# A transformer block on one core: first loads, tables, shared buffers and engine order laid out anew

## The chip, the cores and the metric

The kernel runs on one core of a Trainium2 chip. The core has engines that work side by side and wait for each other through semaphores: TensorE (PE in the profile, with its weight loads as PEld), VectorE (DVE), ScalarE (ACT), GpSimd (POOL) and SyncE (SP, which issues transfers). Transfers run on 16 DMA engines. The metric is device time in microseconds, and lower is better.

## The reference

The input x has the shape (16, 128, 96, 96) in f32: 16 images of 128 channels and 96 x 96 pixels. It passes one block of channel attention and one feed-forward part with a depthwise convolution:

```
xn1 = layernorm over channels(x)
q, k, v = xn1 @ wq.T, xn1 @ wk.T, xn1 @ wv.T         # 8 heads of 16 channels
q, k = l2norm over the pixels(q), l2norm(k)
attn = softmax(q k^T * 16^-0.5)                      # 16 x 16 for each head
x = x + (attn v) @ wp.T
xn2 = layernorm over channels(x)
h1 = w_in xn2                                        # 128 -> 512 channels
h2 = depthwise 3x3 convolution(h1, w_dw)             # padding 1
h3 = gelu(h2)
x = x + w_out h3                                     # 512 -> 128 channels
```

All of it is in f32.

## The kernel before

The channels lie on the 128 partitions, the pixels along the free axis. An image is cut into 8 bands of 12 rows (BR), a band into 3 units of 4 rows (UPB units of UR rows). The 512 hidden channels are 4 chunks of 128.

For each image there is a first pass (names with `_a`): a band of x is loaded (`load`, SP), turned to pixels x channels by PE transposes (`forth`), DVE takes the statistics (`stats`), POOL turns the variance into the factor of the layer norm (`variance`, `power`), the pixels are scaled (`scaled`, by POOL, or for the first image by DVE straight from PSUM, `direct`), PE sums the Gram matrix (`gram`), and the scaled pixels are turned back into the ring buffer xn (`back` on PE, `place` on ACT). `attention` makes from the Gram matrix one 128 x 128 matrix mwT for the image in a chain of short steps over PE, ACT, DVE and POOL. The second pass (`_b`) multiplies xn by mwT (`mix`), adds x, takes the layer norm again and writes xn.

`conv_job` is one chunk of one band: PE makes the hidden rows (`hidden`), ACT copies them to SBUF (`kept`), ACT multiplies the rows by some taps into pr buffers (`products`), POOL adds one of these to the shifted rows in the tile merged (`merge`), DVE runs the other taps into the accumulator acc and at last into an h3 buffer (`tap`), two DMAs that accumulate, issued by POOL, add the remaining products (`add_products`, `add_h3`), and ACT takes the gelu in place. In some bands the fourth chunk runs on PE instead (`by_tiles`, 32 x 32 blocks with the diagonal matrices diag). `ffn_out` multiplies the four h3 tiles of a band by woutT (in the tiled bands by woutR, which is woutT's last chunk with its quarters turned by the unit) and adds the result to x, which SP stores.

The buffers that rotate are h3 (8), pr (8), x1 (2), xb (5), zT (4) and the four PSUM banks h. Before the first images' work, `weights` loads the weights into two h3 buffers, transposes them on PE and makes the tables on DVE: wqkT, wqk2c, winT, woutT, woutR, ratio, eye, diag, ksum, turned.

The order on each engine is written out by the program before anything is issued. Every operation is put on record with `op(engine, ns, place, work, reads, writes, ...)`; `Plan.order` runs them through a model with the durations ns and the places (the constants AT and RANK), which gives a list for each engine and each kind of buffer that several engines take; the table MOVES then shifts single entries of these lists by some positions, and `in_turn` merges the lists into one sequence. On the chip each engine takes its instructions in that sequence and waits where it must. At the start before, the order on SP's queue is: band 0 of x (L1632), wq and wk (L1486, L1487), wp (L1488), w_in, w_out (L1489, L1490), bands 1 to 5, the depthwise weights (L1586), band 6; on ACT's queue stand the four columns w1, b1, w2, b2 (L1324) and wv (L1331).

Of the kernel before, what the change touches and what calls it, by code (L numbers as in the profile page):

```python
# [36 lines left out]
FOURTH_TAP = 6  # L37
LAST_TAP, TOP_LAST, END_LAST = 8, 6, 2
# [11 lines left out]
H3_BUFS = 8  # L50
# [7 lines left out]
    load_w=-10068.713, weights=-247.64243, zeros=-5822.3994, load_a=-41.673394, forth_a=-1466.3766,  # L58
# [2184 lines left out]
```

## Time and profile before

| | |
|---|---|
| median of 3 runs | 3874.92 us (3870.5 to 3881.82) |
| the profiled execution, time | 3873.51 us |
| its span, first to last instruction | 3871.5 us |
| mean granted TensorE clock | 0.991 |
| busy, PE / DVE / ACT / POOL | 3701.4 / 3707.3 / 3570.9 / 3291.6 us |
| DMA, packets' time as a share of 16 engines | 81.2% (issued by POOL), 11.1% (issued by SP) |
| median time to land of an accumulating DMA | 7.4 us (into pr), 7.7 us (into h3) |

How to read the rows: `0.80 0.38 SPq L1632 DMA_DIRECT2D x<-in_x_dram x1` is an instruction at 0.80 us that took 0.38 us, on SP's queue, from line 1632, which writes x from the input; in square brackets stands how long its engine had been idle before it, and what ended that. A row of waits gives the total in us, how many there were, and the longest. A row of groups gives the count, then the busy time in us with the mean of one in ns, then the idle time before them. A row of a stretch gives its two ends and its length, the busy us of PE, PEld, DVE, ACT and POOL with the number of instructions, the granted clock, the busy share of the DMA engines and their GB/s. "issue" is time in which nothing that the profile shows was waited for.

### The profile page before, as it was taken

Reading aid. Unit: us, or ns where it says so; the run is one execution under the profiler, and the core shown is the slowest. Engines: PE = TensorE matmul, PEld = TensorE weight load, DVE = VectorE, ACT = ScalarE, POOL = GpSimd, SP = SyncE. Lnnn points to the kernel's source line nnn. Section 1 sums busy time; section 2 is a strip of 40 time slices with the busy share of each in tenths; the row PEclk is TensorE's granted clock in tenths of the full one; section 3 lists DMA queues with packets and bytes.
Section 4 is the critical chain, followed back from the end, with each engine's and each line's share of the span. In section 5 each row is a group of like instructions: output and inputs, shape, how many; then the busy total and the mean of one; then the engine's idle time right before and its main releaser. Section 6 shows DMA issues by size and latency. Waiting matters only on the chain. (4 is left out here: it accounts for less than half of the span.)

```text
span 3871.5 us, 73795 instructions
## 1 busy us (share of the span) xinstructions
PE 3701.4 (96%) x28244; PEld 2380.4 (61%) x28244; DVE 3707.3 (96%) x4242; ACT 3570.9 (92%) x5444; POOL 3291.6 (85%) x3053
## 2 busy tenths in 40 slices
PE   8999999999999999999999999999999999999987
PEld 6566666666666656656666666666666566665554
DVE  6999999999999999999999999999999999999997
ACT  2999999999999999999999999999999999999995
POOL 5888889898898888889888898898989888887674
PEclk9999999999999999999999999999999999999998
DMA  2799999999999989999999999999999999988996
GB/s 95 166 200 210 188 207 216 197 205 204 206 203 206 195 185 223 192 195 200 197 215 198 196 208 196 200 204 205 203 190 207 196 210 201 204 186 182 198 195 145
DMA packets 186593, 757.62 MB, mean 196 GB/s; under 512 B 21632, under 2 KB 23040, under 8 KB 186240
## 3 DMA queue, kind: packets, MB, share of 16 engines
q0 software_dynamic: 146736, 601.10, 81.2%
q1 hardware_dynamic: 38784, 151.75, 11.1%
q8 instruction: 221, 3.62, 0.4%
q14 instruction: 132, 1.08, 0.1%
q10 hardware_dynamic: 720, 0.07, 0.0%
HBM read 148.85 MB, written 75.50 MB: 58 GB/s over the span
## 5 line engine op out<-in xcount | busy, mean ns | idle before, releaser
L2015 ACT ACTIVATE pr<-h,ratio 128x1152 f32<-128x1152 f32 x1440 | 1785.8, 1280 | 12.8 <-POOL merged L2018 3.5
L2031 DVE SCALAR_TENSOR_TENSOR acc<-h,ratio,acc 128x1152 f32<-128x1152 f32 (+1 forms) x1248 | 1731.9, 1388 | 15.3
L2018 POOL TENSOR_TENSOR merged<-pr,h 128x1152 f32<-128x1152 f32 x448 | 1158.1, 2585 | 137.2 <-ACT pr L2015 85.3
L1999 PE MATMUL h<-xn,winT 128*128 128x384 f32 (+2 forms) x3072 | 1191.6, 495 | 38.5 <-ACT h L2004 14.1
L2151 PE MATMUL h<-h,woutT 128*128 128x384 f32 x2688 | 993.0, 489 | 11.7 <-ACT h L2048 8.1
L2004 ACT COPY h<-h 128x384 f32<-128x384 f32 (+2 forms) x1536 | 717.5, 498 | 77.0 <-PE h L1999 70.7
L1999 PEld LDWEIGHTS h<-xn,winT 128*128 128x128 f32 x3072 | 534.8, 190 | 393.0 <-ACT h L2004 44.8
L2151 PEld LDWEIGHTS h<-h,woutT 128*128 128x128 f32 x2688 | 492.9, 190 | 336.1 <-issue 27.3
L2027 DVE SCALAR_TENSOR_TENSOR acc<-h,ratio,merged 128x1152 f32<-128x1152 f32 x448 | 664.6, 1483 | 25.2 <-POOL merged L2021 10.8
L2027 DVE SCALAR_TENSOR_TENSOR h<-h,ratio,acc 128x1152 f32<-128x1152 f32 x448 | 630.5, 1407 | 12.1 <-PE h L2151 3.1
L2048 ACT ACTIVATE h<-h,ksum 128x1152 f32<-128x1152 f32 (+2 forms) x560 | 588.1, 1080 | 48.7 <-DMA h<-pr 48.4
L2043 POOL DMA_DIRECT2D h<-pr x448 | 466.6, 1044 | 168.1 <-DVE h L2027 36.8
L2040 POOL DMA_DIRECT2D pr<-pr x448 | 469.4, 1066 | 75.2 <-ACT pr L2015 53.0
L2115 PE MATMUL h<-h,diag 32*32 32x384 f32 x13824 | 479.4, 489 | 20.2 <-issue 14.5
L2115 PEld LDWEIGHTS h<-h,diag 32*32 32x32 f32 x13824 | 278.9, 103 | 175.4 <-issue 76.0
L1722 POOL TENSOR_TENSOR ve_a<-ve_a,mhalf 128x4 f32<-128x4 f32 x288 | 359.9, 1253 | 9.4
L1746 POOL TENSOR_TENSOR zT<-zT,ve_a 128x512 f32<-128x512 f32 x270 | 357.4, 1337 | 4.2
L1705 PE MATMUL h<-ident,x 128*128 128x128 f32 x2244 | 330.7, 275 | 29.5 <-DMA x<-in_x_dram 15.7
L1722 POOL TENSOR_TENSOR ve_b<-ve_b,mhalf 128x4 f32<-128x4 f32 x288 | 351.4, 1238 | 6.7
L1705 PEld LDWEIGHTS h<-ident,x 128*128 128x128 f32 x2244 | 266.3, 141 | 147.1 <-issue 55.1
L1655 PE MATMUL h<-xn,mwT 128*128 128x384 f32 x768 | 296.8, 498 | 7.1 <-ACT h L2004 3.4
L1753 PEld LDWEIGHTS g<-zT 128*128 128x128 f32 x2160 | 273.2, 191 | 47.0 <-POOL zT L1746 8.0
(185 smaller groups left out, 4109.9 us busy)
## 6 DMA issues: line engine op xcount, KB each, us to landing
pr<-pr POOLq DMA_DIRECT2D x448, 576.0 KB, 7.4
h<-pr POOLq DMA_DIRECT2D x448, 576.0 KB, 7.7
x<-in_x_dram SPq DMA_DIRECT2D x128, 576.0 KB, 6.5
out_dram<-x SPq DMA_DIRECT2D x127, 576.0 KB, 4.4
x<-in_x_dram POOLq DMA_DIRECT2D x123, 576.0 KB, 6.6
out_dram<-x SPq DMA_DIRECT2D x3, 192.0 KB, 3.0
h<-in_L_conv_w_in_dram SPq DMA_DIRECT2D x1, 256.0 KB, 3.5
h<-in_L_conv_w_out_dram SPq DMA_DIRECT2D x1, 256.0 KB, 3.6
```

Source lines behind the costliest of these rows:

```text
L1705: nc.tensor.transpose(d["pT", q][:, k, :], xt[:, j * P : (j + 1) * P], ident)
L1722: nc.gpsimd.tensor_tensor(rstd, rstd, mhalf, ALU.pow)
L1999: nc.tensor.matmul(rows(ph), lhsT=winT[:, n, :], rhs=window(xn, r0 + r, e - r, 1), start=True, stop=True)
L2004: nc.scalar.copy(window(h1_, r, e - r, 1), rows(d.pop(("ph", r))))
L2015: nc.scalar.activation(to, shifted(t), AF.Copy, scale=ratio[:, n, t : t + 1])
L2018: nc.gpsimd.tensor_tensor(merged, d["pr", dma_taps[0]], shifted(UNIT), ALU.add)
L2027: nc.vector.scalar_tensor_tensor(to, shifted(t), ratio[:, n, t : t + 1], also, ALU.mult, ALU.add)
L2031: nc.vector.scalar_tensor_tensor(to, shifted(t)[:, lo:hi, cut], ratio[:, n, t : t + 1], to, ALU.mult, ALU.add)
L2040: nc.gpsimd.dma_start(out=d["pr", dma_taps[1]], in_=d["pr", t], accum_op=ALU.add)
L2048: nc.scalar.activation(h3, h3, AF.Gelu, bias=ksum[:, z, n : n + 1])
L2115: nc.tensor.matmul(d[s][quads[to], lo:hi, cut], lhsT=diag[quads[of], t, :], rhs=window(h1_, s * UR + dy + lo, hi - lo, dx)[quads[of], :, : ...
L2151: nc.tensor.matmul(rows(d["po"]), lhsT=woutR[:, s, :] if n == PE_CHUNK and by_pe(g) else woutT[:, n, :], rhs=h3s[g, n][:, s * UR : (s + 1) ...
```

## The change

- First loads. The four columns and wv go from ACT's queue to SP's. The weights' loads are split in two operations: `loads_qkp` (wq, wk, wp, wv, w1, b1; one h3 buffer) and `loads` (w2, b2, w_in, w_out; the other), with a place of its own for the second (`load_f`). Bands 5 to 7 of the first image are loaded into pr buffers and no longer into the two x1 buffers. The planner's extra time for the very first load (T_START) goes.
- Tables. eye, diag, turned, woutT and woutR are made by ACT and no longer by DVE, in operations of their own (`diagonals`, `turn_bias`, and `keep_out` as an ACT operation). woutR has two units and no longer three: the first one is woutT itself. ncq is gone: the operation that added it works it out.
- Shared buffers. centre lies in the free part of an h3 buffer; merged becomes a pool `mg` with one buffer.
- h3 has nine buffers and no longer eight.
- A tap on POOL is written (`pool_tap`), with POOL_TAPS empty.
- MOVES is new for every engine and for the lists h and h3, and the lists pr and x1 come in, since more than one engine now takes pr buffers.

```diff
+POOL_TAPS = ()
+MG_BUFS = 1
-H3_BUFS = 8
+H3_BUFS = 9
 AT = dict(
+    load_f=-385.2,
...
 MOVES = dict(
...
-    SP={2: -2, 6: -2, 8: -1, 36: -1, 40: -1, 52: -1, 56: -1, 60: -1, 99: -1, 104: -1, 106: -1, 120: -1, 133: -1,
...
+    SP={0: 2, 4: -1, 6: 6, 9: -1, 10: -3, 12: -3, 37: -1, 43: -1, 53: -1, 57: -1, 61: -1, 69: -1, 73: -1, 91: -1,
...
+    x1={1: -1},
+    xb={3: -1},
+    pr={0: 2, 10: -1, 13: -2, 14: -1, 17: 0, 19: -3, 20: 0, 21: -2, 22: 2, 28: 2, 34: -1, 37: -1, 40: -1, 41: 3,
...
-    xb={1: -1},
-    h3={3: -2, 7: -3, 8: -2, 9: -1},
+    h3={0: 6, 1: 4, 5: -2, 6: 2, 7: -5, 9: -8, 10: -3, 18: -1, 42: -1, 50: -1, 58: -1, 105: -1, 114: -1, 154: -1,
...
-T_START = 2300
+T_POOL_TAP = 2600
...
-    centre = const.tile([P, P], F32, name="centre")
-    nc.vector.tensor_scalar(centre, ident, -1.0 / C, None, ALU.add)
...
-        nc.scalar.dma_start(out=t, in_=v.rearrange("(c o) -> c o", o=1))
+    def column(t, v):
+        nc.sync.dma_start(out=t, in_=v.rearrange("(c o) -> c o", o=1))
...
-    nc.scalar.dma_start(out=wv_sb, in_=wv)
-    ncq = const.tile([1, P], F32, name="ncq")
-    woutR = const.tile([P, UPB, P], F32, name="woutR")
+    woutR = const.tile([P, UPB - 1, P], F32, name="woutR")
-    merged = h1p.tile([P, BR, W], F32, name="merged")
+    mg_bufs = [h1p.tile([P, BR, W], F32, name=f"mg_{k}") for k in range(MG_BUFS)]
...
         def loads():
+            column(w2, ln2_w)
+            column(b2, ln2_b)
+            nc.sync.dma_start(out=v["win"], in_=w_in.rearrange("(n p) c kh kw -> p n (c kh kw)", p=P))
+            nc.sync.dma_start(out=v["wout"], in_=w_out.rearrange("c j kh kw -> c (j kh kw)"))
+        def loads_qkp():
...
+            v["centre"] = b[:, 8 * P : 9 * P]
             nc.sync.dma_start(out=v["wqk"][:, :P], in_=wq)
             nc.sync.dma_start(out=v["wqk"][:, P:], in_=wk)
             nc.sync.dma_start(out=v["wp"], in_=wp)
+            nc.sync.dma_start(out=wv_sb, in_=wv)
+            column(w1, ln1_w)
+            column(b1, ln1_b)
...
+        def diagonals():
             for q in quads:
-                nc.vector.tensor_copy(eye[q, :], ident[q, q])
+                nc.scalar.copy(eye[q, :], ident[q, q])
             for t in range(9):
-                nc.vector.tensor_scalar(diag[:, t, :], eye, ratio[:, PE_CHUNK, t : t + 1], None, ALU.mult)
+                nc.scalar.activation(diag[:, t, :], eye, AF.Copy, scale=ratio[:, PE_CHUNK, t : t + 1])
...
+        def turn_bias():
             for s in range(UPB):
                 for to, of in zip(quads, turn(s)):
-                    nc.vector.tensor_copy(turned[to, s, :], ksum[of, :, PE_CHUNK])
+                    nc.scalar.copy(turned[to, s, :], ksum[of, :, PE_CHUNK])
 
         def keep_out(pt):
-            nc.vector.tensor_copy(woutT.rearrange("p n c -> p (n c)"), pt)
-            for s in range(UPB):
+            nc.scalar.copy(woutT.rearrange("p n c -> p (n c)"), pt)
+            for s in range(1, UPB):
                 for to, of in zip(quads, turn(s)):
-                    nc.vector.tensor_copy(woutR[to, s, :], pt[of, PE_CHUNK * P : (PE_CHUNK + 1) * P])
+                    nc.scalar.copy(woutR[to, s - 1, :], pt[of, PE_CHUNK * P : (PE_CHUNK + 1) * P])
...
-        op("SP", 1700, at("load_w", p), loads, [], mine, 2500, dma=2 * T_MOVE)
+        op("SP", 2700, at("load_w", p), loads_qkp, [], mine[1:], 2500, dma=T_MOVE)
...
+        op("SP", 1800, at("load_f", p), loads, [], mine[:1], 2500, dma=2 * T_MOVE)
+        act(2900, at("late", p), diagonals, [("w", "unit")], [("w", "diag")])
+        act(2400, at("late", p), turn_bias, [("w", "sum")], [("w", "diag")])
...
-        return "xb" if second or i == 0 and b < XB_BUFS else "x1"
+        return "xb" if second or i == 0 and b < XB_BUFS else "x1" if i else "pr"
...
-            nc.vector.tensor_add(v["sqn"], v["ps_r"][:, :P], ncq)
+            nc.vector.scalar_tensor_tensor(v["sqn"], cqk[:, :P], float(NTOK), v["ps_r"][:, :P], ALU.mult, ALU.add)
...
-                rows(d["po"]), lhsT=woutR[:, s, :] if n == PE_CHUNK and by_pe(g) else woutT[:, n, :],
+                rows(d["po"]), lhsT=woutR[:, s - 1, :] if s and n == PE_CHUNK and by_pe(g) else woutT[:, n, :],
```

More of the change, by code (lines that the diff above doesn't have):

```diff
@@ L57 @@
 AT = dict(
-    load_w=-10068.713, weights=-247.64243, zeros=-5822.3994, load_a=-41.673394, forth_a=-1466.3766,
+    load_f=-385.2, load_w=-10068.713, weights=-247.64243, zeros=-5822.3994, load_a=-41.673394, forth_a=-1466.3766,
     stats_a=14511.788, variance_a=8052.0351, power_a=-10117.23, pool_product=152.05, merge=-2414.1489,
@@ L1320, in tile_restormer_block @@
     nc.gpsimd.memset(mhalf, -0.5)
-    def column(v, name):
-        t = const.tile([P, 1], F32, name=name)
-        nc.scalar.dma_start(out=t, in_=v.rearrange("(c o) -> c o", o=1))
-        return t
-    w1, b1 = column(ln1_w, "w1"), column(ln1_b, "b1")
-    w2, b2 = column(ln2_w, "w2"), column(ln2_b, "b2")
+    w1, b1, w2, b2 = (const.tile([P, 1], F32, name=name) for name in ("w1", "b1", "w2", "b2"))
+    def column(t, v):
+        nc.sync.dma_start(out=t, in_=v.rearrange("(c o) -> c o", o=1))
     wv_sb = const.tile([P, P], F32, name="wv_sb")
-    nc.scalar.dma_start(out=wv_sb, in_=wv)
     dw = const.tile([P, NCH, 9], F32, name="dw")
@@ L1413, in tile_restormer_block @@
     plan = Plan(
-        tr=TR_BANKS, bk=BK_BANKS, h=H_BANKS, g=1, batch=BATCHES, zT=ZT_BUFS, x1=X1_BUFS, xb=XB_BUFS, pr=PR_BUFS, h3=H3_BUFS
+        tr=TR_BANKS, bk=BK_BANKS, h=H_BANKS, g=1, batch=BATCHES, zT=ZT_BUFS, x1=X1_BUFS, xb=XB_BUFS, pr=PR_BUFS, h3=H3_BUFS, mg=MG_BUFS
     )
@@ L1479, in loads @@
         def loads():
-            a, b = (flat(h3_bufs[plan.slot["h3", ("weights", k)]]) for k in range(2))
+            a = flat(h3_bufs[plan.slot["h3", ("weights", 0)]])
             v["win"] = a[:, :HID].rearrange("p (n c) -> p n c", c=P)
-            v["wout"], v["wp"] = a[:, HID : 2 * HID], a[:, 2 * HID : 2 * HID + P]
-            v["wqk"], v["wqkT"] = b[:, : 2 * P], b[:, 2 * P : 4 * P]
+            v["wout"] = a[:, HID : 2 * HID]
+            column(w2, ln2_w)
[3 more added lines that the diff above has]
+        def loads_qkp():
+            b = flat(h3_bufs[plan.slot["h3", ("weights", 1)]])
+            v["wqk"], v["wqkT"], v["wp"] = b[:, : 2 * P], b[:, 2 * P : 4 * P], b[:, 4 * P : 5 * P]
             v["wt"] = b[:, 4 * P : 8 * P].rearrange("p (t c) -> p t c", c=P)
-            v["w1centre"], v["wvT"], v["twos"] = b[:, :P], b[:, P : 2 * P], b[:1, 8 * P :]
+            v["w1centre"], v["wvT"], v["twos"] = b[:, :P], b[:, P : 2 * P], b[:1, 4 * P : 5 * P]
+            v["centre"] = b[:, 8 * P : 9 * P]
             nc.sync.dma_start(out=v["wqk"][:, :P], in_=wq)
@@ L1488, in loads, with transposed @@
             nc.sync.dma_start(out=v["wp"], in_=wp)
-            nc.sync.dma_start(out=v["win"], in_=w_in.rearrange("(n p) c kh kw -> p n (c kh kw)", p=P))
-            nc.sync.dma_start(out=v["wout"], in_=w_out.rearrange("c j kh kw -> c (j kh kw)"))
-        def transposed(kind, parts, kept, gives):
+            nc.sync.dma_start(out=wv_sb, in_=wv)
+            column(w1, ln1_w)
+            column(b1, ln1_b)
+        def transposed(kind, of, parts, ns, kept, gives, add=None):
             key = ("weights", next(names))
@@ L1501, in forth @@
                     nc.tensor.transpose(d["pt"][:, k * P : (k + 1) * P], part, ident)
-            pe(440, at(kind, p), forth, mine, [h])
-            dve(700, at(kind, p), lambda: kept(d["pt"]), [h], [("w", g) for g in gives] + mine[1:])
+            pe(440, at(kind, p), forth, mine[of : of + 1], [h])
+            (add or dve)(ns, at(kind, p), lambda: kept(d["pt"]), [h], [("w", g) for g in gives] + (mine[1:] if of else []))
         def keep_qkp(pt):
+            nc.vector.tensor_scalar(v["centre"], ident, -1.0 / C, None, ALU.add)
             nc.vector.tensor_copy(v["wqkT"], pt[:, : 2 * P])
@@ L1511, in keep_qkp @@
             nc.vector.tensor_copy(v["wvT"], pt[:, 3 * P :])
-            nc.vector.tensor_scalar(v["w1centre"], centre, w1, None, ALU.mult)
+            nc.vector.tensor_scalar(v["w1centre"], v["centre"], w1, None, ALU.mult)
         def centred():
             pc = v["pc2"] = bank(("weights", "centred"))
-            nc.tensor.matmul(pc[:, : 2 * P], lhsT=centre, rhs=wqkT, start=True, stop=True)
+            nc.tensor.matmul(pc[:, : 2 * P], lhsT=v["centre"], rhs=wqkT, start=True, stop=True)
             nc.tensor.matmul(pc[:, 2 * P : 3 * P], lhsT=v["wvT"], rhs=v["w1centre"], start=True, stop=True)
@@ L1530, in keep_centred @@
             nc.vector.tensor_tensor(wqk2c, v["ptwos"], wqkT, ALU.mult)
-            nc.vector.tensor_scalar(ncq, cqk[:, :P], float(NTOK), None, ALU.mult)
         def biases():
@@ L1546, in units @@
                 nc.vector.tensor_scalar(ratio[:, n, :], dw[:, n, :], per_unit[:, n : n + 1], None, ALU.mult)
+        def diagonals():
             for q in quads:
-                nc.vector.tensor_copy(eye[q, :], ident[q, q])
+                nc.scalar.copy(eye[q, :], ident[q, q])
             for t in range(9):
-                nc.vector.tensor_scalar(diag[:, t, :], eye, ratio[:, PE_CHUNK, t : t + 1], None, ALU.mult)
+                nc.scalar.activation(diag[:, t, :], eye, AF.Copy, scale=ratio[:, PE_CHUNK, t : t + 1])
         def centred_in():
             pc = v["pc3"] = bank(("weights", "centred in"))
-            nc.tensor.matmul(pc, lhsT=centre, rhs=winT.rearrange("p n c -> p (n c)"), start=True, stop=True)
+            nc.tensor.matmul(pc, lhsT=v["centre"], rhs=winT.rearrange("p n c -> p (n c)"), start=True, stop=True)
             pk = v["pk"] = bank(("weights", "shift"))
@@ L1586, in load_dw @@
             nc.sync.dma_start(out=dw, in_=w_dw.rearrange("(n p) o kh kw -> p n (o kh kw)", p=P))
-        op("SP", 1700, at("load_w", p), loads, [], mine, 2500, dma=2 * T_MOVE)
-        op("SP", 400, at("load_dw", p), load_dw, [], [("w", "dw")], 10000)
-        dve(1400, at("units", p), units, [mine[0], ("w", "dw")], [("w", "in")])
+        op("SP", 2700, at("load_w", p), loads_qkp, [], mine[1:], 2500, dma=T_MOVE)
+        op("SP", 450, at("load_dw", p), load_dw, [], [("w", "dw")], 10000)
         transposed(
-            "weights", lambda: [v["wqk"][:, :P], v["wqk"][:, P:], v["wp"], wv_sb], keep_qkp, ["qk"]
+            "weights", 1, lambda: [v["wqk"][:, :P], v["wqk"][:, P:], v["wp"], wv_sb], 1900, keep_qkp, ["qk"]
         )
@@ L1600, in weights @@
         pc, p2 = ("h", ("weights", "centred")), ("h", ("weights", "twos"))
-        pe(1000, at("weights", p), centred, [("w", "qk"), mine[1]], [pc])
-        pe(440, at("weights", p), twos, [("w", "qk")], [p2])
-        dve(1300, at("weights", p), keep_centred, [pc, p2], [("w", "qk")])
-        dve(700, at("late", p), unit_parts, [mine[0], ("w", "in")], [mine[1]])
+        pe(1500, at("weights", p), centred, [("w", "qk"), mine[1]], [pc])
+        pe(700, at("weights", p), twos, [("w", "qk"), mine[1]], [p2])
+        dve(2000, at("weights", p), keep_centred, [pc, p2], [("w", "qk")])
+        op("SP", 1800, at("load_f", p), loads, [], mine[:1], 2500, dma=2 * T_MOVE)
+        dve(1900, at("units", p), units, [("w", "dw")], [("w", "unit")])
+        act(2900, at("late", p), diagonals, [("w", "unit")], [("w", "diag")])
+        dve(1200, at("late", p), unit_parts, [mine[0], ("w", "unit")], [mine[1]])
         transposed(
-            "late",
+            "late", 1,
             lambda: [v["wt"][:, n, :] for n in range(NCH)],
-            keep_in, ["in"],
+            1400, keep_in, ["in"],
         )
         pc, pk = [("h", ("weights", "centred in"))], [("h", ("weights", "shift"))]
-        pe(1200, at("late", p), centred_in, [("w", "in"), mine[1]], pc + pk)
-        dve(3600, at("late", p), keep_centred_in, pc + pk, [("w", "in")])
+        pe(2000, at("late", p), centred_in, [("w", "in"), mine[1]], pc + pk)
+        dve(2800, at("late", p), keep_centred_in, [*pc, *pk, ("w", "unit")], [("w", "in"), ("w", "sum")])
+        act(2400, at("late", p), turn_bias, [("w", "sum")], [("w", "diag")])
         transposed(
-            "late",
+            "late", 0,
             lambda: [v["wout"][:, n * P : (n + 1) * P] for n in range(NCH)],
-            keep_out, ["out"],
+            2600, keep_out, ["out"], act,
         )
     def x_key(i, b, second):
-        return "xb" if second or i == 0 and b < XB_BUFS else "x1"
+        return "xb" if second or i == 0 and b < XB_BUFS else "x1" if i else "pr"
     def x_band(i, b):
@@ L1629, in go @@
         def go():
-            pool, of = (xpool, xbs) if key == "xb" else (x1pool, x1s)
-            of[i, b] = pool.tile([P, BR * W], F32, tag="x", name=f"x_{i}_{b}")
+            of = xbs if key == "xb" else x1s
+            if key == "pr":
+                of[i, b] = flat(pr_bufs[plan.slot["pr", (i, b)]])
+            else:
+                of[i, b] = (xpool if key == "xb" else x1pool).tile([P, BR * W], F32, tag="x", name=f"x_{i}_{b}")
             nc.sync.dma_start(out=of[i, b], in_=x_band(i, b))
-        move(p, go, [], [(key, (i, b), s) for s in range(UPB)], T_MOVE, 0 if i or b else T_START)
+        move(p, go, [], [(key, (i, b), s) for s in range(UPB)], T_MOVE, 0)
     def norm(i, second, place_of):
@@ L2017, in merge @@
         def merge():
+            merged = d["merged"] = mg_bufs[plan.slot["mg", jn]]
             nc.gpsimd.tensor_tensor(merged, d["pr", dma_taps[0]], shifted(UNIT), ALU.add)
         def merge_too():
-            nc.gpsimd.tensor_tensor(merged, merged, d["pr", dma_taps[3]], ALU.add)
+            if pool_tap is None:
+                nc.gpsimd.tensor_tensor(d["merged"], d["merged"], d["pr", dma_taps[3]], ALU.add)
+            else:
+                nc.gpsimd.scalar_tensor_tensor(
+                    d["merged"], shifted(pool_tap), ratio[:, n, pool_tap : pool_tap + 1], d["merged"], ALU.mult, ALU.add
+                )
         def tap(t):
@@ L2025, in tap @@
                 to = h3_of(g, n) if t == left[-1] else acc
-                also = acc if t == left[-1] else merged if dma_taps else shifted(UNIT)
+                also = acc if t == left[-1] else d["merged"] if dma_taps else shifted(UNIT)
                 nc.vector.scalar_tensor_tensor(to, shifted(t), ratio[:, n, t : t + 1], also, ALU.mult, ALU.add)
@@ L2058, in conv_job @@
             dma_taps = (*dma_taps, FOURTH_TAP)
+        pool_tap = FOURTH_TAP if len(dma_taps) == 3 and 0 < b < NB - 1 and any(n == c and g % of in gs for c, of, gs in POOL_TAPS) else None
         by_pool = dma_taps[0] if third and any(n == c and g % of in gs for c, of, gs in POOL_THIRDS) else None
-        left = [ahead, *(t for t in range(9) if t not in (ahead, UNIT, behind, *dma_taps)), behind]
+        left = [ahead, *(t for t in range(9) if t not in (ahead, UNIT, behind, pool_tap, *dma_taps)), behind]
         h1 = [("h1", n, k) for k in range(4)]
@@ L2078, in conv_job @@
         if dma_taps:
-            pool(T_MERGE, at("merge", j), merge, [*h1, pr[0]], [("merged", 0)], True)
+            pool(T_MERGE, at("merge", j), merge, [*h1, pr[0]], [("mg", jn)], True)
             if len(dma_taps) > 3:
-                pool(T_MERGE, at("merge", j), merge_too, [pr[3]], [("merged", 0)], True)
+                pool(T_MERGE, at("merge", j), merge_too, [pr[3]], [("mg", jn)], True)
+            if pool_tap is not None:
+                pool(T_POOL_TAP, at("merge", j), merge_too, h1, [("mg", jn)], True)
         for k, t in enumerate(left):
-            r = [*h1, ("merged", 0)] if k == 0 and dma_taps else h1
+            r = [*h1, ("mg", jn)] if k == 0 and dma_taps else h1
             w = all_acc if k < len(left) - 1 else h3
@@ L2129, in by_tiles @@
                 n * TAP_NS + PART_NS, at("conv", j + STEP["conv_part"] * k), lambda taps=taps: products(taps),
-                [*h1, ("w", "in")], pcs, 4 * n * UPB * len(quads), JOIN if k else 0,
+                [*h1, ("w", "in"), ("w", "diag")], pcs, 4 * n * UPB * len(quads), JOIN if k else 0,
             )
@@ L2135, in by_tiles @@
             ns = sum(t_act((y - x) * W, 1) for x, y, _ in row_parts(b, s * UR, (s + 1) * UR))
-            act(ns, at("conv_gelu", j), lambda s=s: gelu(s), [pcs[s], ("w", "in")], [("h3", (g, PE_CHUNK), s)])
+            act(ns, at("conv_gelu", j), lambda s=s: gelu(s), [pcs[s], ("w", "in"), ("w", "diag")], [("h3", (g, PE_CHUNK), s)])
     def ffn_out(p, g, s):
```

15 lines of the change are left out of this document (9 added, 6 removed), and 1816 rows, old and new, of tables (ACT, DVE, PE, POOL).

## The prediction

> **What bounds the kernel now.** I read the page's busy times first, then a table of stages, then the start and the waits of each engine.
>
> ```profile
> span 3871.5 us, 73795 instructions
> PE 3701.4 (96%) x28244; PEld 2380.4 (61%) x28244; DVE 3707.3 (96%) x4242; ACT 3570.9 (92%) x5444; POOL 3291.6 (85%) x3053
> ```
>
> PE and DVE are both busy for 96% of the span, so no single engine can be relieved to great effect; what is left is where both stand still. The table by stretches says where that is.
>
> ```profile
> core 0: us, PE busy (x) PEld busy (x) DVE busy (x) ACT busy (x) POOL busy (x), PEclk, DMA share, GB/s
> 0.00:6.40 6.40, 1.18 (x6) 1.14 (x6) 0.57 (x3) 1.47 (x2) 2.11 (x30) 1.00 0.47 127
> 6.40:20.00 13.60, 6.68 (x30) 4.14 (x28) 5.78 (x18) 0.00 (x0) 2.69 (x6) 1.00 0.87 302
> 20.00:60.00 40.00, 35.26 (x285) 32.57 (x284) 35.69 (x120) 9.84 (x21) 22.54 (x42) 0.96 0.15 46
> 60.00:100.00 40.00, 38.03 (x244) 30.51 (x245) 24.71 (x62) 14.16 (x33) 26.56 (x41) 0.96 0.20 60
> 100.00:3837.00 3737.00, 3603.25 (x27645) 2303.11 (x27643) 3630.53 (x4033) 3540.66 (x5382) 3236.01 (x2934) 0.99 0.95 199
> 3837.00:3871.50 34.50, 17.01 (x43) 8.94 (x41) 10.00 (x11) 4.80 (x7) 1.74 (x2) 0.75 0.40 120
> ```
>
> Of DVE's 164 us of idle time 33.3 lie in the first 100 us, 24.5 in the last 34.5 and 106.5 in the 3737 us between, where its idle share is 2.8%, PE's 3.6%, ACT's 5.3%, and the DMA engines are 95% taken. The middle is a balance of four resources. The start is different: ACT is busy there for 25.5 of 100 us, and PE waits for data.
>
> ```profile
> PE acc L1705 <- DMA x<-in_x_dram: 6.2, 1, 6.2
> PE h L1705 <- DMA x<-in_x_dram: 5.2, 1, 5.2
> PE h L1878 <- DVE woutR L1579: 2.2, 1, 2.2
> PE h L1801 <- DVE h L1726: 2.0, 1, 2.0
> ```
>
> These are PE's longest waits up to 62 us (total, times, longest). The 5.2 is the first band's own flight and stays. The 6.2 is the second band, which arrives late because of what SP issues ahead of it:
>
> ```profile
> 0.80 0.38 SPq L1632 DMA_DIRECT2D x<-in_x_dram  x1
> ...
> 5.22 1.09 PE L1705 MATMUL h<-ident,x 128*128 128x128 f32 x4 [5.22 <-DMA x<-in_x_dram]
> 5.28 0.33 SPq L1488 DMA_DIRECT2D h<-in_L_conv_wp_dram  x1
> 5.65 0.43 SPq L1489 DMA_DIRECT2D h<-in_L_conv_w_in_dram  x1
> 6.13 0.50 SPq L1490 DMA_DIRECT2D h<-in_L_conv_w_out_dram  x1
> 6.68 2.83 SPq L1632 DMA_DIRECT2D x<-in_x_dram  x5
> SPq L1488 <- DMA w<-in_L_conv_ln_w_dram: 3.1, 1, 3.1
> 13.94 1.97 PE L1705 MATMUL acc<-ident,x 128*128 128x128 f32 x8 [6.21 <-DMA x<-in_x_dram]
> ...
> 99.18 1.26 ACT L2015 ACTIVATE pr<-h,ratio 128x1152 f32<-128x1152 f32 x1
> ```
>
> Eight transfers (three on SP, five on ACT's queue) leave by 2.7 us; the ninth stands 3.1 us until an early one has landed, and bands 1 to 5 leave only from 6.68, behind 576 KB of weights (wp, w_in, w_out: 64, 256 and 256). Band 1 is first used at 13.94.
>
> **The change, part by part.**
>
> *First loads.* Read by hand from the places and the moves of the SP, x1, xb and pr lists, the new order is band 0, band 1, then wq, wk, wp, wv, w1, b1, then bands 3, 2, 4, with w_in, w_out, w2, b2 and the depthwise weights among the later loads. The eight that leave at once now hold both first bands. Band 0 landed 4.4 us after its issue (0.80 to 5.22); band 1, issued about 0.4 us after it, shares the engines with it, and 1.18 MB at the 302 GB/s of the second stretch take 3.9 us, so it is there by 6.5 to 7.5, just when PE is through with band 0 and the four weight transposes. The 6.2 goes almost whole: -6.2 (ends: -2, if the weights take the bandwidth first, and -6.5). What is late next: bands 3, 2, 4 leave at about 5.3 when band 0 lands, one every 0.5 us, and PE, busy for 35.3 us of the 40 in which it works through seven of them, needs about 5 us for each, so they are in time. The wait of SP also counts its own issues: w1, b1, w2, b2 and wv come from ACT's queue to SP's, five at the 0.33 to 0.50 us of SP's rows above, 2.1 us of SP, hidden by that wait. Bands 5 to 7 go into pr buffers, free until the first products at 99 us: nothing for bands 5 and 6, and band 7 no longer waits for an x1 buffer. Its cover is that the products' order in the pr list comes after.
>
> *Tables.* These leave DVE or shrink:
>
> ```profile
> L1579 DVE COPY woutR<-h 32x128 f32<-32x128 f32 x12 | 3.4, 286 | 0.1
> L1573 DVE COPY turned<-ksum 32x3 f32<-32x3 f32 x12 | 1.9, 160 | 0.2
> L1550 DVE TENSOR_SCALAR diag<-eye,ratio 128x32 f32<-128x32 f32 x9 | 1.4, 235 | 0.0
> L1548 DVE COPY eye<-ident 32x32 f32<-32x32 f32 x4 | 0.7, 178 | 0.0
> L1576 DVE COPY woutT<-h 128x512 f32<-128x512 f32 x1 | 0.7, 674 | 0.0
> ```
>
> Together 8.1 us of DVE; ncq's one short instruction goes too (folded into the operation that read it), and is left at 0. Four of the woutR copies are gone, the rest goes to ACT. There I price it from ACT's own rows of the start:
>
> ```profile
> L1742 ACT COPY zT<-h 128x512 f32<-128x512 f32 x10 | 5.7, 587 | 22.4 <-PE h L1705 16.9 <-DVE st_b L1713 5.6
> L1937 ACT ACTIVATE h<-h,rn 128x128 f32<-128x128 f32 x1 | 0.4, 351 | 0.0
> L1962 ACT COPY mwT<-h 128x128 f32<-128x128 f32 x1 | 0.3, 265 | 0.0
> L1963 ACT COPY d<-h 128x1 f32<-128x1 f32 x1 | 0.2, 166 | 0.0
> ```
>
> woutT 0.59; eight woutR copies at 0.265, 2.1; nine diag at most 0.35, 3.1; sixteen small copies at about 0.17, 2.7: 8.5 us, in a stretch where ACT is idle 74.5 of 100 us. Cover gone, that is if all of it stood in front of a copy to xn that PE waits for, it would cost those 8.5; so the bounds are 0 and +8.5, and I take 0, because ACT's idle is nine times as long. centre moves to a later place on DVE (0.35 us, the same instruction): 0.
>
> On the path, what 8.1 us less DVE is worth is limited by PE, which loses no work: in 20 to 60 us PE is idle for 4.7 us, of which the two rows above give 2.2 (the attention's first product waits for DVE's last woutR copy) and 2.0 (a transpose waits for DVE's scaling). I take -3.5; ends 0 and -8.1, the second if PE could follow DVE in full.
>
> ```profile
> 60.87 0.67 PE L1878 MATMUL h<-wqkT,gs 128*128 128x256 f32 x2 [2.22 <-DVE woutR L1579]
> ```
>
> The Trainium skill, page "ScalarE: Activation LUTs", section "Rules for kernel authors", speaks against the move: it gives plain arithmetic (add, mul, max) to VectorE and not to ScalarE, as up to about three times faster per element, though it says so of bf16. Here the data are f32 and the rows disagree, 0.587 us on ACT against 0.674 on DVE for 128x512; by the rule ACT would need some 25 us, and the start would gain nothing, a time near 3866.
>
> *Ninth h3 buffer.* DVE's last tap, which takes the buffer, waits in the middle as follows (100 to 3837 us):
>
> ```profile
> DVE st_b L1713 <- PE h L1705: 14.3, 18, 2.5
> DVE x L2162 <- PE h L2151: 14.1, 22, 2.3
> DVE acc L2027 <- POOL merged L2021: 10.8, 15, 2.0
> DVE xn L1805 <- PE h L1801: 9.1, 14, 1.5
> ...
> DVE h L2027 <- PE h L2151: 3.1, 7, 0.8
> ```
>
> The last row is that wait: -3 at most by this row, 0 if something else is late next; I take -2.
>
> *Engine order.* Every engine's list of moves is new over the whole run, not at the start alone, and is some 10 to 20% longer; no row shows what it gives. Bounds: the four waits at the head of the last fence, 48 us, are for work that another order could have had ready; all of them gone is -48, and as much again lost is +48. The near row is the shares: with DVE at 97.2%, PE at 96.4% and the DMA engines at 95%, filling one gap opens another, so I take a seventh, -7.
>
> *Nothing.* The merged buffer becomes a pool of one with the same users; the tap on POOL is written but its list is empty; woutR is indexed by s-1. 0 each. T_START, T_POOL_TAP and the new durations are figures of the planner and act through the order alone. The tail:
>
> ```profile
> 3851.98 1.65 PE L2151 MATMUL h<-h,woutT 128*128 128x384 f32 x2 [6.45 <-ACT h L2048]
> ```
>
> These are the last products, behind a last accumulating transfer and its gelu, which the edits leave as they are: 0.
>
> *Sum.* -6.2 -3.5 -2 -7 = -18.7: the span goes from 3871.5 to 3852.8. The profiled execution took 3873.51, 2.0 over its span, and stands 1.4 below the median of the runs, 3874.92. So 3852.8 + 2.0 + 1.4 = 3856.
>
> **The rivals.** A difference below 0.3%, 12 us here, is about what a measurement of this kernel can't tell from none.
>
> *Only the start gains.* The new order is worth no more than the old, because the middle is full. -9.7 and the h3 buffer at 0 give 3865, within 0.3%. If the first bands also come no earlier than the weights let them (-2) and DVE's relief brings the 2.2 of the attention's wait alone, it is 3871. For it: the balance of four resources. Against: the same lists are searched with a buffer more.
>
> *Slower.* Place: ACT's gelu, which waits for the accumulating transfer into h3.
>
> ```profile
> ACT h L2048 <- DMA h<-pr: 38.3, 36, 4.0
> h<-pr POOLq DMA_DIRECT2D x448, 576.0 KB, 7.7
> ```
>
> ACT takes its work in order, so behind a late gelu stand the copies of the next hidden rows, PE's products, and the taps. Now 36 of 448 gelus wait, 1.06 us each. If the new order puts the accumulating transfers closer together, on DMA engines that are 95% taken, landing grows past the distance that the order allows for. With the start's -9.7, twenty more waits (21 us) bring the run to 3886, about +0.3%; from there it is slower, and with as many again 3907. For it: the slack is small and the transfers' landing isn't constant. Against: a ninth buffer lets a tile wait longer for its transfer, which allows more distance, not less.
>
> *The order gives far more.* Two thirds of the 48 us: -9.7 -2 -32 give 3831. For it: those waits are single ones of up to 2.5 us, not the rhythm of the work, so an order without most of them is conceivable; against: PE, DVE and the DMA engines would all have to come to above 98%.
>
> **How the numbers follow.** The forecast (start and a part of the middle, 3845 to 3863) has 0.50; only the start, 0.27; slower, 0.09; far more, 0.14. The forecast and "far more" are faster, with a little of neither on the edge: faster 0.65, within 0.3% 0.26, slower 0.09. The range reaches from 3830, where "far more" lies, to 3876, which takes in the second of the rival "only the start" and the order's first losses.
>
> **What would show it.** Right: the first transposes of band 1 by 8 us instead of 13.94; no wait of over 2 us for x after the first; woutR, diag, eye and turned on ACT, and DVE's sum in the first 60 us smaller by some 8; the attention's first product near 50 us instead of 60.87; the first product tile of the first convolution near 89 instead of 99.18; DVE's idle between there and the tail at about 97 us instead of 106.5; the row of the last tap waiting for the output's product gone. Wrong: band 1 still late; ACT's copies to xn waiting behind the tables and PE behind them; DVE idle over 120 us in the middle, with the gelu's wait for its transfer above 55 us. The prediction rests most on the order's -7, which is the term with the least behind it.

## The result, and the profile after

The changed kernel takes 3851.2 us (median of 6 runs, 3844.64 to 3857.3) where the kernel before takes 3872.34 us (6 runs, 3868.95 to 3881.82): a ratio of 0.9942, 95% interval 0.9926 to 0.9959. It is faster by 21 us; the forecast was 3856 and the range 3830 to 3876. Two later sets of five runs of the same kernel gave 0.9933 (0.9921 to 0.9946) and 0.9933 (0.9919 to 0.9947). The execution profiled here took 3857.3 us, the slowest of its six, so its span is 16 us shorter than before and not 21.

The page's head and the same six stretches as before (the last two shifted by the 16.2 us):

```profile
span 3855.3 us, 73787 instructions
PE 3690.5 (96%) x28244; PEld 2375.7 (62%) x28244; DVE 3697.7 (96%) x4202; ACT 3578.8 (93%) x5479; POOL 3297.7 (86%) x3053
...
0.00:6.40 6.40, 1.25 (x6) 1.28 (x7) 0.00 (x0) 1.67 (x3) 2.22 (x32) 1.00 0.73 229
6.40:20.00 13.60, 10.80 (x55) 8.72 (x54) 9.56 (x30) 0.00 (x0) 7.14 (x12) 0.87 0.95 327
20.00:60.00 40.00, 39.57 (x340) 37.38 (x340) 26.87 (x77) 22.40 (x70) 24.10 (x42) 1.00 0.11 36
60.00:100.00 40.00, 38.73 (x230) 28.93 (x229) 33.56 (x69) 20.58 (x37) 31.85 (x44) 1.00 0.24 62
100.00:3820.80 3720.80, 3581.56 (x27577) 2289.59 (x27576) 3616.59 (x4017) 3528.87 (x5364) 3230.65 (x2923) 0.99 0.96 200
3820.80:3855.30 34.50, 18.58 (x47) 9.79 (x45) 11.08 (x12) 5.28 (x9) 1.74 (x2) 0.77 0.38 107
```

Between 6.4 and 20 us PE is busy for 10.8 us where it was 6.7, and between 20 and 60 us it stands still for 0.4 us where it was 4.7: from 20 us on the start is now PE's. DVE has 13 us of room in the same 40 us, and ACT carries more than twice what it did. In the middle, DVE is idle for 104.2 us where it was 106.5. The tail is as it was, with the same wait of 6.45 us for the last gelu.

SP's first issues and PE's longest waits up to 62 us, after:

```profile
0.80 0.86 SPq L1805 DMA_DIRECT2D x<-in_x_dram  x2
1.71 0.42 SPq L1648 DMA_DIRECT2D h<-in_L_conv_wq_dram  x1
...
4.14 0.43 SPq L1484 DMA_DIRECT2D b<-in_L_conv_ln_b_dram  x1
5.03 2.36 SPq L1805 DMA_DIRECT2D x<-in_x_dram  x3
7.44 0.67 SPq L1805 DMA_DIRECT2D pr<-in_x_dram  x1
...
11.33 0.74 SPq L1639 DMA_DIRECT2D h<-in_L_conv_w_in_dram  x1
PE acc L1878 <- DMA x<-in_x_dram: 5.2, 1, 5.2
PE h L1698 <- DVE h L1671: 1.0, 1, 1.0
PE acc L1878 <- DVE h L1899: 0.9, 1, 0.9
PE h L1878 <- DMA x<-in_x_dram: 0.3, 1, 0.3
```

Two bands leave at once, then the six transfers for the first tables, and the next bands at 5.03, when the first has landed. The wait of 6.2 us for the second band is gone:

```profile
6.88 1.06 PE L1878 MATMUL h<-ident,x 128*128 128x128 f32 x4
...
13.29 0.44 PE L1878 MATMUL h<-ident,x 128*128 128x128 f32 x2 [0.30 <-DMA x<-in_x_dram]
```

PE takes the second band's first transposes at 6.88 us, by its order of work, right behind those of the first band and without a wait. The 0.3 us in the list of waits are for a later band, at 13.29 us. The tables, on ACT:

```profile
L1740 ACT COPY turned<-ksum 32x3 f32<-32x3 f32 x12 | 2.3, 192 | 0.1
L1746 ACT COPY woutR<-h 32x128 f32<-32x128 f32 x8 | 2.1, 257 | 0.1
L1715 ACT ACTIVATE diag<-eye,ratio 128x32 f32<-128x32 f32 x9 | 2.0, 307 | 0.0
L1713 ACT COPY eye<-ident 32x32 f32<-32x32 f32 x4 | 0.9, 214 | 0.0
L1743 ACT COPY woutT<-h 128x512 f32<-128x512 f32 x1 | 0.6, 601 | 0.0
```

Together 7.9 us, in ACT's idle time. The attention's first product and the first product tile of the first convolution are the milestones that the prediction named:

```profile
50.53 0.60 PE L2051 MATMUL h<-wqkT,gs 128*128 128x256 f32 x2
...
L2188 ACT ACTIVATE pr<-h,ratio x1440: 1236/1267/1600, 87.1 to 3811.0; 128x1152 f32<-128x1152 f32 x180
```

The second row, like those of its kind below, is the summary of the product tiles pr: the two times in it are the starts of the first and the last one. 60.87 has become 50.53, and 99.2 has become 87.1: the start is 12.1 us shorter.

In the middle DVE's longest waits are now

```profile
DVE st_b L1886 <- PE h L1878: 26.5, 31, 3.2
DVE xn L1978 <- PE h L1974: 10.0, 18, 1.9
DVE x L2344 <- PE h L2333: 7.2, 14, 1.4
DVE acc L2206 <- POOL mg L2196: 7.1, 11, 1.4
...
PE h L1878 <- DMA x<-in_x_dram: 21.3, 18, 3.4
```

(the last row is PE's, over the same stretch). The wait of the last tap for the output's product (3.1 us before) is gone from the list; the wait of x + output for the output's product has halved and that for merged has shrunk, and in their place DVE waits longer for the transposes of the second pass, and PE longer for bands of x (9.8 us in the same stretch before).

### The profile page after: what moved, and what is told of

The parts are those of the page before. It is cut to its first block, busy times and chain, and to the rows that moved or that the text cites. A ratio compares the mean times of both kernels' runs of the same rounds, so it can differ in the third digit from the quotient of the medians.

```text
span 3855.3 us, 73787 instructions
## 1 busy us (share of the span) xinstructions
PE 3690.5 (96%) x28244; PEld 2375.7 (62%) x28244; DVE 3697.7 (96%) x4202; ACT 3578.8 (93%) x5479; POOL 3297.7 (86%) x3053
## 4 chain that ended last, share of the span: by engine, by line
PE 44%; DVE 22%; ACT 12%; POOL 9%; DMA 7%; issue 6%; DVEq 0%; ACTq 0%; POOLq 0%
PE h L2172 12%; PE h L2333 11%; DVE acc L2210 10%; PE h L2297 6%; ACT pr L2188 6%; DVE acc L2206 4%; PE g L1926 4%; DMA x<-in_x_dram 4%; PE h L1974 3%; PE h L1828 3%; DVE h L2206 3%; PE h L1878 3%; POOL mg L2192 3%; ACT h L2177 2%; DMA h<-pr 2%
## 5 line engine op out<-in xcount | busy, mean ns | idle before, releaser
L2210 DVE SCALAR_TENSOR_TENSOR acc<-h,ratio,acc 128x1152 f32<-128x1152 f32 (+1 forms) x1248 | 1730.0, 1386 | 14.8
L2192 POOL TENSOR_TENSOR mg<-pr,h 128x1152 f32<-128x1152 f32 x448 | 1173.4, 2619 | 125.6 <-ACT pr L2188 61.6
L2333 PE MATMUL h<-h,woutT 128*128 128x384 f32 x2816 | 1039.3, 489 | 7.0 <-ACT h L2227 6.4
L2333 PEld LDWEIGHTS h<-h,woutT 128*128 128x128 f32 x2816 | 514.3, 191 | 335.4 <-issue 25.7
L2206 DVE SCALAR_TENSOR_TENSOR acc<-h,ratio,mg 128x1152 f32<-128x1152 f32 x448 | 657.5, 1468 | 21.6 <-POOL mg L2196 7.1
L2222 POOL DMA_DIRECT2D h<-pr x448 | 481.3, 1077 | 172.9 <-DVE h L2206 38.3
L1919 POOL TENSOR_TENSOR zT<-zT,ve_a 128x512 f32<-128x512 f32 x270 | 367.3, 1369 | 3.9
L1828 PE MATMUL h<-xn,mwT 128*128 128x384 f32 x768 | 297.4, 496 | 10.2 <-DVE xn L1978 3.5
```

The source lines that it names most:

```text
L2192: nc.gpsimd.tensor_tensor(merged, d["pr", dma_taps[0]], shifted(UNIT), ALU.add)
L2206: nc.vector.scalar_tensor_tensor(to, shifted(t), ratio[:, n, t : t + 1], also, ALU.mult, ALU.add)
L2210: nc.vector.scalar_tensor_tensor(to, shifted(t)[:, lo:hi, cut], ratio[:, n, t : t + 1], to, ALU.mult, ALU.add)
L2222: nc.gpsimd.dma_start(out=h3_of(g, n), in_=d["pr", dma_taps[1]], accum_op=ALU.add)
L2333: nc.tensor.matmul(rows(d["po"]), lhsT=woutR[:, s - 1, :] if s and n == PE_CHUNK and by_pe(g) else woutT[:, n, :], rhs=h3s[g, n][:, s * UR ...
```

## The experiments

All twelve kernels were timed against the kernel before in five rounds, which gave 5 to 12 runs of each. In the kernels whose order is changed, each engine's and each buffer's list is written down and no longer worked out by the planner; the edit is then

```diff
-        return [ops[k][3] for k in self.in_turn(lists)]
+        return [ops[k][3] for k in self.in_turn(stored())]
```

with `stored()` giving the lists named below.

### Start against order, and the ninth buffer

**e1: the new start with the old order.** The changed kernel; the lists are its own for the first 400 operations, then those of the kernel before.

> The changed kernel up to the first convolution's first product (its first 400 operations: loads, tables, nine h3 buffers), and from there on every engine's and buffer's list in the order of the kernel before. Theory 'start': the 12 us that the changed trace shows at the first product tile (99.18 to 87.06) go through to the end, and the middle adds the rest: ratio 0.9965 to 0.9975, about 3860, and the first product at 87. Rival 'order': the start's gain is given back, because the old order was made for the old start; the gain comes from the new order with its ninth buffer: ratio 0.998 to 1.002.

Measured: 0.9943 (0.9931 to 0.9955), median 3854.2.

**e2: the old start with the new order.** The kernel before with `H3_BUFS = 9` and, to make room for the buffer, the room edits (centre in the free part of an h3 buffer, eight woutR copies for twelve, ncq folded in); its own lists for the first 397 operations, then those of the changed kernel.

```diff
-H3_BUFS = 8
+H3_BUFS = 9
-    centre = const.tile([P, P], F32, name="centre")
-    ncq = const.tile([1, P], F32, name="ncq")
-    woutR = const.tile([P, UPB, P], F32, name="woutR")
+    woutR = const.tile([P, UPB - 1, P], F32, name="woutR")
...
+            nc.vector.tensor_scalar(v["centre"], ident, -1.0 / C, None, ALU.add)
...
```

> The kernel before up to the first convolution (its first 397 operations; loads and tables on their old engines and in their old order), then the lists of the changed kernel, with nine h3 buffers. To make room for the ninth, centre, woutR's first unit and ncq are placed as in the changed kernel, still made by DVE. Theory 'start': the gain without the start's 12 us is left, ratio 0.997 to 0.998, about 3863, first product near 99. Rival 'order': the whole gain, ratio 0.994 to 0.9955, about 3853.

Measured: 0.9945 (0.9931 to 0.9959), median 3851.3.

**e3: nine buffers in the kernel before**, with the same room edits and its own lists.

> The kernel before with its own order on every engine and a ninth h3 buffer (room made as in the run before this one). Theory 'start': the wait of the last tap for the output's product (3.1 us) goes, ratio 0.9985 to 1.0. Rival 'buffer': the ninth buffer is what the middle's gain comes from, ratio 0.996 to 0.998. If an order made for eight buffers cannot use the ninth: 1.0.

Measured: 0.9970 (0.9958 to 0.9982), median 3865.4.

**e4: the changed kernel on the same chip.**

> The changed kernel itself, on the same chip as the three others: ratio 0.993 to 0.996 by both theories; start and order together.

Measured: 0.9933 (0.9921 to 0.9946), median 3847.4.

The first products of e1 to e4:

```profile
L2188 ACT ACTIVATE pr<-h,ratio x1440: 1237/1267/1439, 86.8 to 3808.4; 128x1152 f32<-128x1152 f32 x180
L2012 ACT ACTIVATE pr<-h,ratio x1440: 1235/1267/1488, 94.9 to 3805.6; 128x1152 f32<-128x1152 f32 x180
L2012 ACT ACTIVATE pr<-h,ratio x1440: 1233/1267/1462, 95.6 to 3809.9; 128x1152 f32<-128x1152 f32 x180
L2188 ACT ACTIVATE pr<-h,ratio x1440: 1237/1266/1585, 86.3 to 3800.5; 128x1152 f32<-128x1152 f32 x180
```

Neither theory in its pure form holds: the new start alone and the new order alone each come near the whole gain, because both include the ninth buffer and the room edits, which give 0.3% by themselves. That the first product of e2 and e3 is at 95 and not at 99 is in part the room edits' doing and in part that of TensorE's granted clock, which was 1.00 over their first 80 us and 0.96 in the profiled execution before (more on this in the last section).

**e5: the room edits with eight buffers**, in the kernel before.

> The kernel before with the room edits alone (centre in an h3 buffer, eight woutR copies for twelve, ncq folded in) and eight h3 buffers, in its own order: what of the 0.997 of the run with nine buffers is the buffer's. Theory 'buffer': the edits give the 3.6 us seen at the first product tile (99.2 to 95.6) and no more, ratio 0.9985 to 0.9995, and the ninth buffer gives the other 6 to 8. Rival 'edits': all of it, 0.996 to 0.998, and the buffer nothing beyond its 3.1 us of wait.

Measured: 0.9984 (0.9973 to 0.9995), median 3867.3 (12 runs); the first product at 96.7:

```profile
L2012 ACT ACTIVATE pr<-h,ratio x1440: 1237/1267/1446, 96.7 to 3822.8; 128x1152 f32<-128x1152 f32 x180
PE h L1875 <- DVE woutR L1576: 1.1, 1, 1.1
```

The second row is the attention's wait for DVE's woutR copies, 1.1 us with eight of them where it was 2.2 with twelve. Edits and buffer share the 0.3%. With eight buffers the new order was not tried: its lists take a ninth h3 buffer before they give one back, so they cannot be laid on eight.

### The parts of the start

**e6: the weights' loads ahead of the second band again.** Changed kernel; in SP's list both weight operations stand directly behind the first band, and they come first in the list of h3.

> The changed kernel with SP's weight loads (all ten transfers) put back between the first and the second band of x, and all else as it is. Theory 'the second band is the path': the first product tile comes 5 to 7 us later than 86.3 to 87.1, and the end 4 to 7 later, ratio 0.9945 to 0.9955 against 0.993 to 0.994. Rival 'hidden': the first product within 2 us of 87, ratio unchanged.

Measured: 0.9946 (0.9928 to 0.9964), median 3854.3.

**e7: the tables on DVE again.**

```diff
-                nc.scalar.copy(eye[q, :], ident[q, q])
+                nc.vector.tensor_copy(eye[q, :], ident[q, q])
...
-            2600, keep_out, ["out"], act,
+            2600, keep_out, ["out"],
```

and so for diag, turned, woutT and woutR; the three operations stand in DVE's list where they fell by the old sequence.

> The changed kernel with eye, diag, turned, woutT and woutR (eight copies) on DVE again, at the same place among DVE's operations. By the prediction (-3.5, limited by PE): first product at 90, ratio 0.9940 to 0.9950. If DVE is the path in full: 7 us, first product at 93 to 94, ratio 0.995. Rival: DVE in the new start has room (it was busy for 26.9 us of 40 between 20 and 60): first product within 2 us of 87, ratio unchanged.

Measured: 0.9934 (0.9917 to 0.9950), median 3847.0. At the first product, below, it is the forecast that holds, and in the time the rival's "unchanged". PE waits for DVE again, here for the scaling of pixels, where the changed kernel's list has no such row:

```profile
PE g L1926 <- DVE h L1899: 2.6, 1, 2.6
```

**e8: both undone.**

> Both of these undone in the changed kernel. If the two parts carry the start's gain: first product at 95 to 99, ratio 0.995 to 0.997. If the rest of the new start's order carries it: first product below 92, ratio 0.9935 to 0.995.

Measured: 0.9944 (0.9925 to 0.9962), median 3853.7. The first products of e6, e7 and e8, and PE's wait for the second band in e6:

```profile
L2188 ACT ACTIVATE pr<-h,ratio x1440: 1234/1267/1582, 91.7 to 3808.2; 128x1152 f32<-128x1152 f32 x180
L2188 ACT ACTIVATE pr<-h,ratio x1440: 1235/1267/1581, 91.1 to 3801.3; 128x1152 f32<-128x1152 f32 x180
L2188 ACT ACTIVATE pr<-h,ratio x1440: 1234/1267/1512, 95.4 to 3816.6; 128x1152 f32<-128x1152 f32 x180
PE h L1878 <- DMA x<-in_x_dram: 6.1, 1, 6.1
```

At the start the two parts are clean and add up: against 86.3 to 87.1, the loads are worth 4.6 to 5.4 us and the tables 4.0 to 4.8. Both together give 8.3 to 9.1 by e8's execution, whose granted clock over the first 80 us was 1.00 where e6, e7 and the two of the changed kernel had 0.98; by executions that agree in this clock (e8 to e10, next section) they give 9.2 to 10.0. At the end, five or six runs could not tell how much of that arrives.

### Once more, with more runs

**e9: the changed kernel**, and **e10: both parts undone** as in e8.

> The changed kernel again, as the measure for the three others of this call: ratio 0.993 to 0.995.

> The changed kernel with the weights' loads ahead of the second band and the tables on DVE, once more, for the question whether the 8.5 us by which its first product is late (95.4 against 86.9) reach the end. Theory 'passes through': 7 to 9 us over the changed kernel of this call. Rival 'absorbed': 3 us or less.

Measured: e9 0.9933 (0.9919 to 0.9947), median 3847.6; e10 0.9962 (0.9949 to 0.9975), median 3861.1. The first products of e9 and e10:

```profile
L2188 ACT ACTIVATE pr<-h,ratio x1440: 1234/1267/1597, 85.5 to 3797.4; 128x1152 f32<-128x1152 f32 x180
L2188 ACT ACTIVATE pr<-h,ratio x1440: 1234/1268/1587, 96.3 to 3815.5; 128x1152 f32<-128x1152 f32 x180
```

At the first product both parts are worth 9.2 to 10.0 us where the clock over the first 80 us was 0.98 (e10 against 86.3 to 87.1), and 9.9 where it was 1.00 (e8 against e9). At the end both are worth 12 us this time (the difference of the means), and over both sets together 7.1 us (3855.9 over 11 runs against 3848.8 over 16, standard errors 1.8 and 1.1). The start's lead passes through to the end within the errors; that it is absorbed is not borne out. This holds for both parts together. Of the tables alone nothing is seen at the end: e7's mean is 3848.1 with a standard error of 1.6, against 3848.8 with 1.1.

**e11: the new start with the old order** as in e1.

> The new start with the old order from the first convolution on, once more: the order's share with everything else equal. By the prediction's term (-7): 6 to 8 us over the changed kernel of this call; by the traces of the middle, where the new order wins and loses by turns and is ahead by 2 us in sum: 1 to 4 over it.

Measured: 0.9951 (0.9939 to 0.9964), median 3855.1, 7 us over e9. Over both sets the new order is worth 4.9 us (3853.7 over 10 runs against 3848.8).

**e12: a spliced order.** The times of the 448 last taps, read from six traces of the new order and two of the old one with nine buffers, showed the new one 5 us slower in two stretches.

> The changed kernel with the old order in two stretches in which six traces of the new order were slower than two of the old, by 5 us each (last taps 84 to 112 and 364 to 392 of the 448, about 800 to 1040 us and 3150 to 3390 us). If these 5 us belong to the stretch: 6 to 10 us under the changed kernel of this call, ratio 0.991 to 0.992, the fastest of all. Rival: the loss in a stretch is work that the new order has taken in early and gets back in the next, so that the splice gains nothing or loses: ratio 0.993 to 0.997.

Measured: 0.9935 (0.9922 to 0.9947), median 3845.8. The splice gains nothing, as the rival said. Times of the last taps, as a lead over the kernel before in us (one profiled execution each):

| last tap | before, at | changed (three executions) | e1 | e12 |
|---|---|---|---|---|
| 0 | 108.7 | 11.9, 12.8, 13.4 | 12.2 | 11.1 |
| 84 | 805.3 | 12.2, 16.1, 15.9 | 10.8 | 8.7 |
| 112 | 1039.4 | 6.8, 9.3, 9.7 | 10.9 | 9.0 |
| 168 | 1511.3 | 14.0, 19.4, 20.3 | 12.3 | 15.2 |
| 364 | 3164.9 | 14.4, 20.4, 25.4 | 11.9 | 16.4 |
| 392 | 3402.6 | 11.5, 21.1, 24.5 | 14.3 | 10.2 |
| 447 | 3843.4 | 14.8, 25.5, 28.4 | 18.2 | 15.3 |

In the first spliced stretch (84 to 112) the loss of 5 to 7 us is indeed gone, but e12 entered it with less of a lead, and in the second (364 to 392) it loses 6 us with the old order. From 112 to 168 the changed kernel gains 7 to 11 us, which fits work taken early and got back later. But e12, which had lost nothing in the stretch before, gains 6 us there too (9.0 to 15.2), so that this is what happens is not shown.

### The sum of the steps

Means of all the runs of each kernel:

| kernel | runs | mean, us | standard error | step |
|---|---|---|---|---|
| before | 43 | 3874.3 | 0.8 | |
| + room edits (e5) | 12 | 3868.2 | 1.3 | -6.1 |
| + ninth buffer (e3) | 5 | 3863.1 | 1.6 | -5.1 |
| + new start (e1, e11) | 10 | 3853.7 | 0.8 | -9.4 |
| + new order = changed (after, e4, e9) | 16 | 3848.8 | 1.1 | -4.9 |

The kernels were timed on more than one occasion; the kernel before was run each time, and its medians lay between 3872.3 and 3874.5. No experiment beat the changed kernel: e7 (3848.1) and e12 (3848.2 in the mean) are equal to it within the errors.

The last two steps depend on which is taken first. By way of e2 (old start, new order, six runs, mean 3853.5, standard error 2.6) the new order is worth 9.6 us with an error of 3.0, and the new start, on top of it, 4.7 with an error of 2.8. The errors are too large to tell the two ways apart. Both together are worth 14.3 us, with an error of 1.9.

## Why the prediction was right, step by step

The forecast was 18.7 us less, in four terms; the measured gain is 21 to 27 by the medians of the three sets, and 25.5 by the means of all runs. The kinds and the places of the gain were right. The terms were not all right in size, and that the sum comes near is in part luck: the room edits, the buffer and (at the first product) the tables gave more than forecast, and the loads, and perhaps the order, less.

- *First loads, -6.2.* Right in kind and place: the second band is there when PE asks for it, and bringing back the old order of SP brings back the wait, 6.1 us (e6). At the first product it is worth 4.6 to 5.4 us, a little under the term; why not the whole wait arrives there was not looked into. The bands behind were in time, as claimed, but for 0.3 us.
- *Tables, -3.5, limited by PE's idle time.* Right in kind, undersized. Moving them to ACT is worth 4.0 to 4.8 us at the first product (e7 against the changed kernel), and four copies of woutR less take another 1.1 us off the attention's wait (2.2 to 1.1, e5). The step that failed is the share of the limit: the prediction took 3.5 of the 4.7 us for which PE was idle between 20 and 60 us, and only 0.4 us of idle time are left there. A fuller clock is not behind it: the changed kernel has a slow stretch of its own, from 16.5 to 20 us (0.51), and the mean granted clock up to 60 us is 0.97 in both. ACT's price was right: 7.9 us against 8.5, and no wait of PE for ACT stands among its longest. At the end of the run e7 shows nothing of this term. Of the Trainium skill's rule for plain arithmetic (page "ScalarE: Activation LUTs", section "Rules for kernel authors") the traces bear out a part, and not the factor of three: the small operations are dearer on ACT than on DVE in e7 (0.307 against 0.236 us for a diag of 128x32, 0.192 against 0.159 for turned), the larger ones cheaper (0.601 against 0.689 for woutT, 0.257 against 0.287 for woutR). Only diag is a multiplication, as the rule has it; the others are copies.
- *Start in all, -9.7.* Measured -10.3 at the attention's first product (60.87 to 50.53) and -12.1 at the first product tile. Behind the attention's first product the granted clock was 0.83 from 60 to 70 us before and 1.00 after, so that the last 1.7 us need not be the change's. At the end the start is worth 9.4 us with the old order (e3 to e1) and 4.7 with the new one (from e2).
- *Room edits, 0 but for the copies.* The prediction left ncq and centre at 0 without a row for it, and counted the four copies less among the tables. With all three edits e5 is 6.1 us faster at the end, with an error of 1.5. Its first product is 2.5 us early (99.2 to 96.7), of which about 1.2 is the clock's by the comparison in the last section, and 1.1 the attention's wait. Where the rest of the 6.1 arises stays open.
- *Ninth buffer, -2, at most -3.* The row of waits that it was read from is gone, as said. The step measures -5.1 with an error of 2.0, so it may be no more than the row of 3.1. Not counted by the prediction was what the buffer is for: the new order needs it.
- *Engine order, -7.* -4.9 with a standard error of 1.4 on top of the new start, -9.6 with 3.0 on top of the old one. It is the term with the least behind it, and it holds in size, not through the waits that bounded it: the four rows together went from 48.3 to 50.8 us. The output's wait has halved (14.1 to 7.2) and merged is down (10.8 to 7.1), while the transposes of the second pass went up (14.3 to 26.5) and PE's wait for x more than doubled. One gap filled opened another, as the prediction said of the middle. The halved wait for the output is the order's own doing: with the same start and buffer and the old order, the output's wait is 15.1 us in e1 and in e11 (100 to 3800 us), and the transposes' 17.3 and 20.0. The prediction's sign, DVE idle for about 97 us in the middle, did not come in the first execution (104.2). From 100 to 3800 us DVE is idle for 105.5 us before, 103.5, 98.3 and 94.5 in three executions of the changed kernel, and 103.4 and 98.7 in e1 and e11, so that this sign doesn't tell the orders apart.
- *The rivals.* "Only the start" (3865) is ruled out by the time; buffer and order have a share each, the order's 3.5 times its error. "Slower" is ruled out by the time too, and by the gelu's wait for its transfer, which did not grow:

```profile
ACT h L2227 <- DMA h<-pr: 29.3, 28, 3.6
```

29.3 us in 28 waits over the middle, against 38.3 in 36.

What the prediction named wrongly: the first band that the old order loads is band 1 of the image and not band 0; nothing hangs on it.

## What to carry to other kernels

Where the steady part is a balance of several engines, look at the start: there one engine waits while another is idle, and the gain can be read off the trace to within a few microseconds; here, within the errors, it stayed to the end. Measure edits that only make room, too: here fewer copies, a table placed elsewhere and one folded instruction were worth as much as the buffer that they made room for. Where two changes are taken in steps, take them in both orders and give the error of each step. A difference between two orders in one stretch says little before the next stretch is looked at too.

## What had not been expected of the hardware

TensorE's granted clock falls to a half for some microseconds in the middle of the work, and not in every execution. In the kernel before it was 0.50 from 42 to 44 us, behind a wait of 2.0 us that ended at 40.15. The eight transposes there take 1.97 us for what takes 1.04 later in the changed kernel. In the changed kernel it was 0.51 from 16.5 to 20 us, and no wait of PE in the 11 us before was longer than 1.0 us:

```profile
42.00:44.00 2.00, 2.00 (x10) 2.00 (x11) 0.54 (x2) 0.00 (x0) 0.00 (x0) 0.50 0.25 39
41.85 1.97 PE L1705 MATMUL acc<-ident,x 128*128 128x128 f32 x8 [0.18 <-DVE h L1726]
...
60.41 1.04 PE L1878 MATMUL h<-ident,x 128*128 128x128 f32 x8
16.50:20.00 3.50, 3.50 (x17) 3.50 (x18) 1.40 (x7) 0.00 (x0) 1.55 (x3) 0.51 1.00 344
```

(The first two rows are from the kernel before, the last two from the changed one.) So the length of the wait alone doesn't decide it; what does, no run shows. The milestones of the start move with it. Six executions share the changed kernel's start, and their first products follow the mean granted clock over the first 80 us:

| execution | granted clock, 0 to 80 us | first product, us |
|---|---|---|
| e9 | 1.00 | 85.5 |
| e4, e1, the changed kernel | 0.98 | 86.3, 86.8, 87.1 |
| e12, e11 | 0.96 | 87.8, 88.1 |

A step of 0.02 goes with about 1.2 us. The kernel before had 0.96, e5 0.98, e2 and e3 1.00, so a difference of one or two microseconds between two traces at the start can be the clock's.

Two executions of the changed kernel with the same start (first products at 87.1 and 86.3) differ by 11.8 us in their spans, 3855.3 and 3843.5, and the difference comes up in the middle, a few microseconds at a time. That is about half of the whole change, so single runs and single traces tell little here; the means above rest on 5 to 43 runs.
